# Pinning the neighbour-list work of a sparse attention layer behind the projection's stores and the attention's own products

## The chip, the cores and the metric

The kernel runs on one core of a Trainium2 chip. The metric is the device time of one execution in microseconds. Before the change the median of three runs is 1817.77 us (1814.16 to 1821.57).

## The reference

One layer of a graph network on 4096 nodes with 512 features and 8 heads, followed by a residual layer norm. The adjacency matrix has about 17 neighbours in a row of 4096.

```python
hs = layer_norm(x, ln1_scale, ln1_bias)             # sources
ht = layer_norm(h_target, ln1_scale, ln1_bias)      # targets
q = (ht @ Wq + bq).reshape(T, H, HD) / sqrt(HD)
k = (hs @ Wk + bk).reshape(S, H, HD)
v = (hs @ Wv + bv).reshape(S, H, HD)
logits = where(adj[None] != 0, einsum('thd,shd->hts', q, k), -1e30)
ctx = einsum('hts,shd->thd', softmax(logits), v).reshape(T, D)
ht = layer_norm(ht + ctx @ Wo + bo, ln2_scale, ln2_bias)
y = ht + gelu(ht @ W1) @ W2                         # 512 -> 2048 -> 512
out = layernorm(x + y)
```

All node masks are one. The kernel checks on the chip that its short lists held all neighbours; if not, a dense path follows, which did not run in the executions shown.

## The kernel before, in words

**Lists.** The 4096 targets are 32 tiles of 128 rows. For each tile `edges(i)` (line 717) turns 128 x 4096 adjacency words into lists of neighbours, in four quarters of 1024 columns. A quarter is loaded by SyncE (line 714, 512 KB). ScalarE takes its Sign into bytes and sums the row's degree (line 729). VectorE multiplies pairs of bytes by a row of column numbers (line 734, here "the mask"), and takes the eight largest of five segments (`max`, line 736). After four quarters a decoding follows on VectorE (lines 743 to 760). Quarters are numbered n = 4 i + h here. Quarters of lists 0 to 19 land in the first eight slots of a ring of gathered rows; later ones in two `wide` buffers, so that a load waits for the Sign two quarters before it. Signs go to three `signs` buffers in turn.

**Sorting.** The targets of each half (16 lists) are sorted by degree (`sort`, lines 808 to 858), and their records are scattered to DRAM by 16 indirect transfers of GpSimd (line 854), so that tiles of the sorted order have nearly equal numbers of neighbours, 11 to 39 slots.

**Projection.** `project` normalizes the sources, transposes them on TensorE and multiplies each tile of 128 by Wk and Wv (line 930, 16 matmuls of 512 columns). ScalarE copies both results to a row tile (line 932) and stores it to the DRAM tensor `kvd` (line 936, a transfer issued by ScalarE's queue). `newest` holds that store's instruction, and `latest` a piece of the last row's tile.

**Attention.** For each tile of the sorted order `front` (line 983 on) gathers the targets and makes q. The neighbours' rows k|v are gathered from `kvd` slot by slot by GpSimd (line 967), up to three slots in a step. A step is: q times k on VectorE (line 1220), the sum over each head, the logits (line 1225), exp on ScalarE (1229 or 1238), v times the weights for two slots on VectorE (line 1184) and for the third on ScalarE (eight products, `by_scalar`, line 1204, whose last one becomes `newest`), and the sum over slots by transposing matmuls on TensorE (line 1192). `finish` normalizes and projects by Wo; for a group of two tiles it ends in `h2T` (line 1147). The groups are one tile, then 15 pairs, then one tile.

**Feed-forward.** `feed(g)` multiplies by W1 (line 1325), takes gelu (1328) and multiplies by W2 (1334) once the group's h2T is there, while attention goes on with the next group. `end` does the last layer norm, and GpSimd scatters the rows out (line 1302).

**What sets the order.** The parts are Python generators, woven by `_weave`: each yields a cost, and the one with the least sum goes on. A yield of `None` means that the generator waits. In the first weave there are the projection (7.8 a row), the first half's lists with their sort (2 a quarter, 4 a decoding) and `fill`, which starts once the first half is through and makes five lists of the second half. In the second weave there are attention (60 a pair of tiles in all), feed-forward (60 a pair), and `other_lists`, which begins at 40 and goes on with the remaining 11 lists at 1.5 times those costs, then sorts the second half. This gives the order in which the instructions are written. The framework then puts the instructions of each engine in an order of its own: by when it reckons that their operands are there, and by the written order among those that are ready. An instruction whose operands come early can so be moved far ahead of its place. `tc.issue_after(ins)` forbids that for the instructions written in its block on the engine of `ins`: they are put behind `ins` in that engine's queue. It adds no wait.

Of the kernel before, what the change touches and what calls it, by code (L numbers as in the profile page):

```python
# [1 line left out]

# [441 lines left out]
def adj_resnorm_kernel(  # L444
# [33 lines left out]
    nc = tc.nc  # L478
# [54 lines left out]
    with tc.tile_pool(name="keep", bufs=1) as keep:  # L533
# [17 lines left out]
        with ExitStack() as late:  # L551
# [157 lines left out]
            def quarter(i, h):  # L709
# [4 lines left out]
                nc.sync.dma_start(a, adj[i * P:(i + 1) * P, h * QW:(h + 1) * QW])  # L714
                return a

            def edges(i):

                part = 1 if i >= NA else 0
                rec = Rs[part][:, i - PARTS[part][0], :]  # L720
                cand = lp.tile([P, SEG, 8], U16, name="cand", bufs=2)
                for h in range(NQ):
                    n = i * NQ + h
                    while len(adjs) < min(n + 2, NT * NQ):
                        adjs.append(quarter(*divmod(len(adjs), NQ)))
                    a, adjs[n] = adjs[n], None

                    sg = turn_of("signs", signs)
                    nc.scalar.activation(sg, a, AF.Sign, accum_out=dpart[:, i, h:h + 1])  # L729
                    ahead = min(n + DEEP - 1, n + 3 + n // 2)  # L730
                    while len(adjs) < min(max(n + 3, min(ahead, RINGED * NQ)), NT * NQ):
                        adjs.append(quarter(*divmod(len(adjs), NQ)))
                    wd = sg.bitcast(U16)
                    nc.vector.tensor_tensor(wd, wd, lio, ALU.mult)
                    for s, (w0, w1) in enumerate(SEGS):
                        nc.vector.max(cand[:, h * SQ + s, :], wd[:, w0:w1])  # L736
                    if h == 1:
                        keep_rest()
                    if h % 2 and moms:
                        moments(moms.pop(0))  # L740
                    yield 2.0
                dec = dec_w
                nc.vector.tensor_single_scalar(dec[:, 0], cand, 255, op=ALU.bitwise_and)
                nc.vector.tensor_single_scalar(dec[:, 1], cand, 8, op=ALU.logical_shift_right)
                gid = lp.tile([P, 2 * SEG, 8], F32, name="gid")
                dec = dec.rearrange("p b s e -> p (b s) e")
                off = segoff.rearrange("p b q s -> p (b q s)")
                nc.vector.scalar_tensor_tensor(gid, dec, 0.0,
                                               off.unsqueeze(2).to_broadcast([P, 2 * SEG, 8]),
                                               op0=ALU.is_gt, op1=ALU.mult)  # L750
                nc.vector.tensor_add(gid, gid, dec)
                flat = gid.rearrange("p s e -> p (s e)")
                for r in range(RE // 8):
                    top = rec[:, E0 + r * 8:E0 + (r + 1) * 8]
                    nc.vector.max(top, flat)  # L755
                    if r + 1 < RE // 8:
                        nc.vector.match_replace(flat, top, flat, 0.0)
                held.append((rest_d[i * P:(i + 1) * P, :], flat))
                has = lp.tile([P, MAXE], F32, name="ehas")
                nc.vector.tensor_scalar(has[:, :RE], rec[:, E0:E0 + RE], 0.0, 0.0, op0=ALU.is_gt,  # L760
                                        op1=ALU.add, accum_out=cnt[:, i:i + 1])
                yield 4.0
# [198 lines left out]
                        yield cost  # L961


            recs, tqs, h2Ts, done, ready, latest, newest = {}, {}, {}, set(), [], [], []

            def gather(dst, table, idx):
                nc.gpsimd.indirect_dma_start(  # L967
# [199 lines left out]
            def attention():  # L1167


                tails, pend = [], []  # L1170

                def advance():
                    go_on()
                    for t in list(tails):
                        if next(t, StopIteration) is StopIteration:
                            tails.remove(t)

                def values(i, j0, n, kv, p, cps, after):

                    m = n - 1 if n == S else n
                    v4 = kv[:, :m, D:].rearrange("p j (h d) -> p j h d", h=H)
                    nc.vector.tensor_tensor(v4, v4, p[:, j0:j0 + m, :].unsqueeze(3)  # L1184
                                            .to_broadcast([P, m, H, HD]), ALU.mult)
                    slots = list(range(n))
                    if m > 1 and i >= NA:
                        nc.vector.tensor_add(kv[:, 0, D:], kv[:, 0, D:], kv[:, 1, D:])
                        slots.remove(1)
                    for j in slots:  # L1190
                        for c in range(KC):
                            nc.tensor.matmul(cps[:, c, :], kv[:, j, D + c * P:D + (c + 1) * P], ident,  # L1192
                                             is_transpose=True, start=j0 + j == 0 and c == 0,
                                             stop=j0 + n == TILES[i][1] and j == slots[-1],
                                             skip_group_check=True)
                    if after is not None:
                        tails.append(after)

                def by_scalar(kv, lg):
                    pa = sp.tile([P, H], F32, name="pa")  # L1200
                    nc.scalar.activation(pa, lg[:, S - 1, :], AF.Exp)
                    for hd in range(H):
                        v = kv[:, S - 1, D + hd * HD:D + (hd + 1) * HD]
                        newest[:] = [nc.scalar.mul(v, v, pa[:, hd:hd + 1]).ins]  # L1204

                request(0)
                yield 0.0
                k = 0
                for group in GROUPS:
                    hs = []  # L1210
                    mv = sp.tile([P, 2, 2], F32, name="mv2")
                    cost = 0.5 * UNIT * len(group) / 2 / sum(TILES[i][1] for i in group)
                    for i in group:
                        cps = ps.tile([P, KC, P], F32, name="cps", bufs=2)
                        while k < len(SG) and SG[k][0] == i:
                            _, j0, n = SG[k]
                            while i not in tqs:
                                step(fronts, i)
                            kv, tq = kvs.pop(k), tqs[i]
                            nc.vector.tensor_tensor(kv[:, :n, :D], kv[:, :n, :D],  # L1220
                                                    tq[:, :D].unsqueeze(1).to_broadcast([P, n, D]),
                                                    ALU.mult)
                            lg = sp.tile([P, S, H], F32, name="lg")
                            latest[:] = [lg[:, 0, 0:1]]
                            nc.vector.tensor_reduce(lg[:, :n, :],  # L1225
                                                    kv[:, :n, :D].rearrange("p j (h d) -> p j h d", h=H),
                                                    AX.X, ALU.add)
                            if j0 > 0:
                                nc.scalar.activation(p[:, j0:j0 + n, :], lg[:, :n, :], AF.Exp)  # L1229
                            advance()  # L1230
                            yield cost * n
                            if pend:
                                values(*pend.pop())
                                request(k)
                            advance()
                            if j0 == 0:
                                p = sp.tile([P, MAXE, H], F32, name="p", bufs=1)
                                nc.scalar.activation(p[:, :n, :], lg[:, :n, :], AF.Exp)
                            if n == S:
                                by_scalar(kv, lg)  # L1240
                            last = j0 + n == TILES[i][1]
                            after = finish(i, p, cps, group, hs, mv) if last else None
                            pend.append((i, j0, n, kv, p, cps, after))
                            yield cost * n
                            k += 1
                values(*pend.pop())
                while tails:
                    advance()
                    yield 3.0
                verdict()  # L1250
# [131 lines left out]
            UNIT = 60.0  # L1382

            ed = all_edges()
            steps = NQ + 1
            both = NG
            order = list(range(NG))
            proj = project(order, first_x)
# [31 lines left out]
            def fill():  # L1420
# [1 line left out]
                while not ready:  # L1422
                    yield None
                yield 9.0
                for cost in _take(ed, FILL * steps):
                    yield cost

            att = attention()
            _weave((projections(), 0), (prepare(), 0), (fill(), 0))
# [57 lines left out]
```

## Time and profile before

| | |
|---|---|
| median of three runs | 1817.77 us |
| profiled execution | 1817.49 us |
| its span, first to last instruction | 1815.5 us |
| TensorE matmuls | 1677.8 us busy (92%) |
| VectorE | 1436.5 us busy (79%) |
| ScalarE | 1224.1 us busy (67%) |
| GpSimd | 982.2 us busy (54%) |
| Signs, line 729 | 128 of 1056 ns, 134.9 us busy; 100.0 us idle before them |
| masks, line 734 | 128 of 411 ns, 52.2 us busy; 21.7 us idle before them |
| maxima, line 736 | 640 of 252 ns, 131.8 us busy |
| granted TensorE clock, mean | 0.967 |

In the profile PE is TensorE's matmuls, PEld its weight loads, DVE is VectorE, ACT ScalarE, POOL GpSimd, SP SyncE; a q after the engine marks its sequencer, which issues transfers and waits. L729 is line 729. A row of the timeline is start, length, engine, line, operation, output and inputs, count, and in brackets the engine's idle time before it and what ended it. A row of windows gives, for a stretch of the span, its length, the busy time of each engine with the number of its instructions, the granted clock as a share, the busy share of the 16 DMA engines and what they moved. Most of the ring's views are named kv, so a Sign reads kv<-kv.

### The profile page before, as it was taken

How to read it: one execution, taken by the hardware profiler on the slowest of the kernel's cores; microseconds unless marked ns; L12 is line 12 of the kernel's file. 1: busy time of each engine (PE TensorE's matmuls, PEld its weight loads, DVE VectorE, ACT ScalarE, POOL GpSimd, SP SyncE). 2: the span in 40 equal slices, each digit the busy share in tenths (PEclk: the TensorE clock that was granted, in tenths of full speed). 3: DMA queues.
4: the chain of work that ended last, by engine and by line, in shares of the span. 5: the costliest groups of instructions: out<-in, count | busy, mean ns of one | idle time of the engine just before them, and what ended most of it. 6: DMA issues, size and time to landing. Idle time of an engine off the chain costs nothing. (4 is left out here: it accounts for less than half of the span.)

```text
span 1815.5 us, 22973 instructions
## 1 busy us (share of the span) xinstructions
PE 1677.8 (92%) x7030; PEld 1097.9 (60%) x7030; DVE 1436.5 (79%) x2660; ACT 1224.1 (67%) x3121; POOL 982.2 (54%) x834
## 2 busy tenths in 40 slices
PE   7989984597999979999999989999999999999997
PEld 3434442465766656766776757666666666666664
DVE  6989876899999837777978989978878797988200
ACT  5767654487987736766778868877777676787311
POOL 1000144656566676766678788867575665763101
PEclk9999996698999989999999999999999999999998
DMA  9999968989887557777878878787776776774000
GB/s 344 366 380 372 344 198 319 404 287 332 271 305 256 201 173 243 258 255 267 273 263 302 293 260 295 249 285 250 241 266 222 248 251 238 244 248 153 18 6 26
DMA packets 140269, 463.26 MB, mean 255 GB/s; under 512 B 16500, under 2 KB 21672, under 8 KB 140136
## 3 DMA queue, kind: packets, MB, share of 16 engines
q0 software_dynamic: 96656, 342.64, 55.8%
q1 hardware_dynamic: 35664, 95.98, 15.0%
q10 hardware_dynamic: 7816, 23.08, 3.3%
q8 instruction: 58, 0.95, 0.2%
q14 instruction: 75, 0.61, 0.1%
HBM read 430.75 MB, written 30.89 MB: 254 GB/s over the span
## 5 line engine op out<-in xcount | busy, mean ns | idle before, releaser
L967 POOL DMA_INDIRECT kv<-kvd,rec x603 | 758.1, 1257 | 347.5 <-PE cps L1192 139.7
L1334 PE MATMUL po<-w,gt 128*128 128x512 f32 x1024 | 466.4, 598 | 16.2 <-ACT gt L1328 16.2
L1325 PE MATMUL pf<-h2T,w 128*128 128x256 f32 (+1 forms) x2176 | 465.9, 368 | 0.1
L1325 PEld LDWEIGHTS pf<-h2T,w 128*128 128x128 f32 x2176 | 389.3, 191 | 64.5 <-issue 20.3
L1220 DVE TENSOR_TENSOR kv<-kv,tq 128x1536 f32<-128x1536 f32 (+2 forms) x211 | 351.6, 1675 | 68.3 <-DMA kv<-kvd,rec 56.2
L1204 ACT ACTIVATE kv<-kv,pa 128x64 f32<-128x64 f32 x1520 | 391.0, 336 | 4.3
L1225 DVE TENSOR_REDUCE lg<-kv 128x24 f32<-128x1536 f32 (+2 forms) x211 | 350.1, 1666 | 1.4
L1334 PEld LDWEIGHTS po<-w,gt 128*128 128x128 f32 x1024 | 188.8, 192 | 212.4 <-issue 194.3
L1192 PEld LDWEIGHTS cps<-ident,kv 128*128 128x128 f32 x2008 | 240.2, 145 | 109.4 <-issue 59.2
L1192 PE MATMUL cps<-ident,kv 128*128 128x128 f32 x2008 | 264.5, 280 | 44.1 <-DVE kv L1184 24.5
L1184 DVE TENSOR_TENSOR kv<-kv,p 128x1024 f32<-128x1024 f32 (+1 forms) x211 | 251.0, 1193 | 22.8 <-ACT p L1229 20.3
L687 POOL TENSOR_TENSOR n_rs<-n_ve,mhalf 128x2 f32<-128x2 f32 (+2 forms) x51 | 50.8, 997 | 329.1 <-DVE n_ve L680 165.3
L729 ACT ACTIVATE kv<-kv 128x1024 uint8<-128x1024 int32 x128 | 134.9, 1056 | 100.0 <-DMA kv<-in_adj_dram 51.7
L1328 ACT ACTIVATE gt<-pf 128x512 f32<-128x512 f32 x128 | 76.4, 597 | 93.8 <-PE pf L1325 75.8
L1328 ACT ACT_TABLE_LOAD x104 | 133.4, 1283 | 1.7
L736 DVE MAX8 cand<-kv 128x8 uint16<-128x103 uint16 (+1 forms) x640 | 131.8, 252 | 0.8 <-DVE R L755 0.2
L930 PE MATMUL pq<-wk,h2T 128*128 128x512 f32 x256 | 120.8, 616 | 12.1 <-ACT tq L932 7.2
L1012 PE MATMUL t<-wq,tq 128*128 128x512 f32 x256 | 118.2, 605 | 5.6 <-ACT tq L1006 5.6
L930 PE MATMUL pq<-wv,h2T 128*128 128x512 f32 x256 | 115.5, 594 | 6.4 <-ACT kv L729 3.0
L1229 ACT ACTIVATE p<-lg 128x24 f32<-128x24 f32 (+2 forms) x179 | 39.2, 219 | 113.0 <-DVE lg L1225 88.8
L1116 PE MATMUL t<-wo,rb 128*128 128x512 f32 x256 | 115.2, 592 | 0.0
L930 PEld LDWEIGHTS pq<-wk,h2T 128*128 128x128 f32 x256 | 48.9, 197 | 69.9 <-issue 55.2
(160 smaller groups left out, 1582.2 us busy)
## 6 DMA issues: line engine op xcount, KB each, us to landing
kv<-in_adj_dram SPq DMA_DIRECT2D x128, 512.0 KB
kvd<-tq ACTq DMA_DIRECT2D x24, 512.0 KB
kv<-kvd,rec POOLq DMA_INDIRECT x603
kv<-in_L_gnn_h_target_dram SPq DMA_DIRECT2D x32, 256.0 KB
kv<-in_x_dram SPq DMA_DIRECT2D x15, 512.0 KB
rest_d<-gid SPq DMA_DIRECT2D x32, 160.0 KB
w<-in_L_gnn_W_dram SPq DMA_DIRECT2D x4, 1024.0 KB
kvd<-kv ACTq DMA_DIRECT2D x8, 512.0 KB
```

The source lines that it names most:

```text
L729: nc.scalar.activation(sg, a, AF.Sign, accum_out=dpart[:, i, h:h + 1])
L736: nc.vector.max(cand[:, h * SQ + s, :], wd[:, w0:w1])
L930: nc.tensor.matmul(pkv, hT[:, kc, j * P:(j + 1) * P], w[:, kc, :], start=kc == 0, stop=kc == KC - 1)
L967: nc.gpsimd.indirect_dma_start(out=dst, out_offset=None, in_=table[:, :], in_offset=bass.IndirectOffsetOnAxis(ap=idx, axis=0))
L1184: nc.vector.tensor_tensor(v4, v4, p[:, j0:j0 + m, :].unsqueeze(3) .to_broadcast([P, m, H, HD]), ALU.mult)
L1192: nc.tensor.matmul(cps[:, c, :], kv[:, j, D + c * P:D + (c + 1) * P], ident, is_transpose=True, start=j0 + j == 0 and c == 0, stop=j0 + n ...
L1204: newest[:] = [nc.scalar.mul(v, v, pa[:, hd:hd + 1]).ins]
L1220: nc.vector.tensor_tensor(kv[:, :n, :D], kv[:, :n, :D], tq[:, :D].unsqueeze(1).to_broadcast([P, n, D]), ALU.mult)
L1225: nc.vector.tensor_reduce(lg[:, :n, :], kv[:, :n, :D].rearrange("p j (h d) -> p j h d", h=H), AX.X, ALU.add)
L1325: nc.tensor.matmul(pf[:, k, :], w1[(f0 + k) // KC][:, kc, (f0 + k) % KC * P:((f0 + k) % KC + 1) * P], h2T[:, kc, :w], start=kc == 0, stop= ...
L1328: nc.scalar.activation(gt, pf, AF.Gelu_apprx_tanh)
L1334: nc.tensor.matmul(po[j], gt[:, k, j * P:(j + 1) * P], w2[(f0 + k) // KC][:, (f0 + k) % KC, :], start=False, stop=f0 + k == FC - 1, skip_g ...
```

## The change

Three things are done. The Sign of a quarter of the second half's lists (16 to 31) is put behind `newest`, the newest k|v store or the last of ScalarE's newest eight products at the point where the Sign is written. Each mask is put behind `logits`, the newest logits instruction (empty until attention is written). And `fill` makes three of its five lists as before, and the other two after the last k|v row has been written. A quarter's step is split in two yields, 1 + 1 for the second half's lists and 0 + 2 for the first half's, so that other work can be written between a Sign and its mask; the counts of steps follow (9 a list in place of 5).

```diff
+            def behind(ins):
+                return tc.issue_after(ins[-1]) if ins else nullcontext()
+
             def edges(i):
...
                     sg = turn_of("signs", signs)
-                    nc.scalar.activation(sg, a, AF.Sign, accum_out=dpart[:, i, h:h + 1])
+                    with behind(newest if i >= NA else []):
+                        nc.scalar.activation(sg, a, AF.Sign, accum_out=dpart[:, i, h:h + 1])
                     ahead = min(n + DEEP - 1, n + 3 + n // 2)
                     while len(adjs) < min(max(n + 3, min(ahead, RINGED * NQ)), NT * NQ):
                         adjs.append(quarter(*divmod(len(adjs), NQ)))
+                    yield 0.0 if i < NA else 1.0
                     wd = sg.bitcast(U16)
-                    nc.vector.tensor_tensor(wd, wd, lio, ALU.mult)
+                    with behind(logits):
+                        nc.vector.tensor_tensor(wd, wd, lio, ALU.mult)
...
-                    yield 2.0
+                    yield 2.0 if i < NA else 1.0
...
-            recs, tqs, h2Ts, done, ready, latest, newest = {}, {}, {}, set(), [], [], []
+            recs, tqs, h2Ts, done, ready, latest = {}, {}, {}, set(), [], []
+            newest, logits = [], []
...
-                            nc.vector.tensor_reduce(lg[:, :n, :],
-                                                    kv[:, :n, :D].rearrange("p j (h d) -> p j h d", h=H),
-                                                    AX.X, ALU.add)
+                            logits[:] = [nc.vector.tensor_reduce(
+                                lg[:, :n, :], kv[:, :n, :D].rearrange("p j (h d) -> p j h d", h=H),
+                                AX.X, ALU.add).ins]
...
-            steps = NQ + 1
+            steps = 2 * NQ + 1
...
-                for cost in _take(ed, FILL * steps):
-                    yield cost
+                yield from _take(ed, (FILL - 2) * steps)
+                while not latest:
+                    yield None
+                yield from _take(ed, 2 * steps)
```

More of the change, by code (lines that the diff above doesn't have):

```diff
@@ L1 @@
-from contextlib import ExitStack
+from contextlib import ExitStack, nullcontext
 import concourse.bass as bass
```

## The prediction

> **What bounds the kernel now.** I read the busy shares first, then the 40 slices, then busy time in windows cut at the events of the start-up, then the timeline of ScalarE and GpSimd around the last k|v row.
>
> ```profile
> PE 1677.8 (92%) x7030; PEld 1097.9 (60%) x7030; DVE 1436.5 (79%) x2660; ACT 1224.1 (67%) x3121; POOL 982.2 (54%) x834
> PEclk9999996698999989999999999999999999999998
> ```
>
> TensorE is busy 92% of the span; 138 us of it are idle. Where they lie, by windows:
>
> ```profile
> core 0: us, PE busy (x) PEld busy (x) DVE busy (x) ACT busy (x) POOL busy (x), PEclk, DMA share, GB/s
> 203.00:291.00 88.00, 67.44 (x176) 29.76 (x174) 68.37 (x291) 51.33 (x97) 23.89 (x27) 0.95 0.76 254
> 291.00:373.00 82.00, 44.00 (x182) 31.59 (x182) 65.70 (x105) 40.05 (x132) 56.28 (x46) 0.68 0.96 364
> 373.00:446.00 73.00, 63.16 (x344) 45.80 (x345) 71.38 (x149) 56.66 (x155) 46.23 (x41) 0.91 0.91 320
> 446.00:571.00 125.00, 123.51 (x561) 86.38 (x561) 123.19 (x279) 109.92 (x269) 68.72 (x57) 1.00 0.83 284
> ```
>
> TensorE loses 20.6, 38.0 and 9.8 us in the first three rows, 68 of its 138. From 446 us, where the second group's h2T (line 1147) is ready and its feed-forward starts, TensorE has 98.8% busy in the fourth row and stays near that to the end (1087 of 1126 us after 690). So a gain has to move that point, 446, which I call X; what moves X moves the end one for one. What sets X is VectorE: its gaps are 19.6, 16.3 and 1.6 us in the three rows, 37.5 in all, and from 337 to 446 it has almost none. All of VectorE's work up to X (205.5 us) is done in order, so X is 203 plus that work plus those gaps.
>
> Now the end of the projection, ScalarE's timeline:
>
> ```profile
> 279.25 1.06 ACT L729 ACTIVATE kv<-kv 128x1024 uint8<-128x1024 int32 x1 [2.39 <-DMA kv<-in_adj_dram]
> 280.21 0.19 ACT L729 ACTIVATION_READ_ACCUMULATOR kv<-kv 128x1 f32 x1
> 280.31 0.56 ACT L932 COPY kv<-pq 128x512 f32<-128x512 f32 x1
> ...
> 288.93 1.06 ACT L729 ACTIVATE kv<-kv 128x1024 uint8<-128x1024 int32 x1 [2.57 <-DMA kv<-in_adj_dram]
> 289.89 0.19 ACT L729 ACTIVATION_READ_ACCUMULATOR kv<-kv 128x1 f32 x1
> 289.99 0.57 ACT L932 COPY kv<-pq 128x512 f32<-128x512 f32 x1
> 290.58 0.33 ACTq L936 DMA_DIRECT2D kvd<-kv  x1
> ```
>
> The copies of k and v (line 932) stand behind Sign operations (line 729) that wait for adjacency to land. Over 203 to 300 us Signs waited 23.3 us for that and 10.0 for VectorE's maxima. Numbering Signs in order of time, quarters 84 to 92 (lists 21 to 23) run before the last k|v store at 290.58, although the code writes them inside the attention loop. The gathers wait for that store:
>
> ```profile
> 292.63 0.95 POOL L967 DMA_INDIRECT xt<-in_x_dram,tags  x1 [0.31 <-issue]
> 296.58 0.94 POOL L967 DMA_INDIRECT kv<-kvd,rec  x1 [3.00 <-DMA rest_d<-gid]
> ```
>
> The releaser named there is only the last to land; a gather reads all of kvd, whose last store left 6.0 us earlier.
>
> [...] the copy at 280.31 starts as the Sign in front of it, which had idled ScalarE for 2.39 us, is done. [...] weight loads are only 69% busy from 446 to 571, so VectorE's 98.6% in that row is as likely a limit, and I count losses there too.
>
> **The change part by part.**
>
> *Nothing is added to compute.* The yields split one step in two of the same total cost; for lists 0 to 15 the first half costs 0, so their order stays. The added dependencies are order only. Instructions added: none, 0 us. No table load comes with a Sign in the trace (no line 729 row of that kind).
>
> *Signs of lists 16 to 20 behind k|v stores.* By the costs of the planner, source row k is written at 7.8 k, the filling lists from 207 on, so quarters 64 to 75 are pinned behind the stores of rows 26 to 30, and lists 19 and 20 (quarters 76 to 83) behind the last, row 31. Before, quarter 64 ran at 203 and quarter 83 at 257. This frees ScalarE for the projection. Unblocked rows took about 7.3 us in TensorE (line 930 groups start at 46.7, 54.4, 61.3, 69.0, 75.9). Row 23 starts at 204.8; row 31 would start at 204.8 + 8 x 7.3 = 263.2, end 7.2 later (16 matmuls, two runs of 3.60), and its store leave at about 271 in place of 290.6: 19.6 earlier. The record chain has room: its 16 scatters run 243 to 263, records load at 268 to 271, targets' rows from 272; without list work in front of the sort it should be some us earlier. I take first gather 6.0 after the store, first product 11.5 after that (296.58 to 308.06 now): 288.5 in place of 308.1. Were the record chain not earlier, the first product would come near 295.
>
> *Loads.* Each load of a quarter needs its buffer, so loads slip with the Signs on SP's queue: nothing else waits there but the 160 KB stores of the rest. Quarters 86 to 97, 12 x 0.5 MB = 6 MB, leave the start-up and go behind it. At the 364 GB/s of the second row that is 16 us of transfer, taken from a stretch where gathers waited 11.0 us in four places, and put where the share is 0.91 to 0.96.
>
> *Signs and masks of lists 21 to 31 behind products and logits.* They start where the code writes them, planner time 40, which is the second product row of tile 1. Before, quarters 84 to 98 had run ahead, 258 to 328 us; by 383 us the lead was used up and lists went at the written pace. Up to X (second h2T, planner time 135) the written order masks quarters up to 105; the trace has 107 by 446.8. So the work before X falls by two quarters. A quarter costs 0.41 (line 734) and 5 x 0.206 (line 736), a list's decoding 132.6/32 = 4.1 us (lines 743 to 760), 2.5 a quarter in all; consecutive instructions overlap, and counted without overlap it is 89 us for 43 quarters, 2.1. Gain: 2 x 2.1 = 4.
>
> *VectorE's gaps after.* From 203 to 288.5 there is work for 20 quarters, 42 us, and the sort and small parts, 9: 34.5 us of gap, 15 more than now up to 291. From there the start-up: 16.3 us of gap now, of which 10.1 lie in 291 to 308 and vanish; of the other 6.2 I keep 4. Then 1.6. Sum 40.1 against 37.5: 2.6 lost. The 19.6 us by which attention starts earlier are thus paid back almost whole: list work that had filled VectorE's empty time moves into its full time.
>
> *Coupling.* Now masks follow Signs by 5 to 10 us (462.43 to 471.3 for quarter 111). After it, a Sign stands behind eight products, so it ends 0.2 + 2.0 + 1.25 = 3.5 us after the logits, and a VectorE at 98% may wait for it at the mask. The trace has no such pair to time. Lower bound 0, the other operations in between (1.2 us values, 1.76 products, 1.74 logits) cover 3.5; upper, 0.5 us for each of 44 quarters, 22 us. I take 0.03 to 0.1 each, 1 to 4, as the cover suffices on paper: 3 us. Queued behind such a mask are products and logits of the next slots, and TensorE's transposes wait for those.
>
> Sum: -4 + 2.6 + 3 = +1.6, less about 2 for fewer load waits of ScalarE between 383 and 456 (9 us there, nearly all covered): 0. The profiled execution took 1817.49 us (span 1815.5 and 2.0 around it), the median of the three runs is 1817.77, so the two bases are the same. I predict 1817. Half a per cent, 9 us, is what a measurement of this kernel can tell from no change.
>
> **Rivals.**
>
> *The start-up gain is kept (faster).* If lists after the change run late against the written order, so that before X VectorE does attention only, the 19.6 us stay, less 3: about 1800. For it: 337 to 373 shows VectorE doing attention alone, and no consumer needs the second half's lists before tile 16, near 1015 us. Against: the pinned masks keep their written rank, and the 446 to 571 row has no free VectorE time to take them later (1.8 us).
>
> *Masks stall VectorE (slower).* In 337 to 571 each of the 44 quarters waits for its Sign, 0.5 us each, 22 us, less the 3 counted: about 1836. It decides from 0.27 us each (12 us). For it: ScalarE is 78 to 88% busy there, with 1.28 us table loads and gelus that wait for TensorE in the same queue. Against: the cover above.
>
> *It does not do what it says:* if the stores are not earlier, since something else holds the last rows, lists still lose their early places; about 1822 to 1830, a part of the slower case. And in the 636 to 690 row 10 us of TensorE time are lost behind the second sort's scatters on GpSimd; another order may shift that by 5 either way.
>
> **How the numbers follow.** No change 0.40 (its own range 1807 to 1828: most of it within 9 us, 0.03 below, 0.04 above), kept gain 0.25, slower by stalls or by stores that are not earlier 0.35, of which 0.02 fall within 9 us. So faster 0.28, same 0.35, slower 0.37. For 8 in 10 the range takes in both other cases' centres: 1795 to 1840.
>
> **What would show it.** The last k|v store near 271 and the first product near 288 show the start-up step; Signs of quarters 84 on after 320 show the pins; X between 440 and 452 shows the repayment; VectorE's waits for line 729 at line 734 (18.9 us now) show the coupling. I am wrong if X moves by over 10 us, or if TensorE's idle after X changes by as much.

## The result and the profile after

The changed kernel takes 1834.42 us (1829.49 to 1835.9) beside 1816.01 for the kernel before in the same comparison: a ratio of 1.0097, 95% interval 1.0076 to 1.0117. Repeated later beside the experiments it took 1825.4, ratio 1.0066 (1.0042 to 1.009). It is slower by 0.7 to 1.0%, where no change was forecast. The profiled execution shown here took 1833.78 us, its span is 1832.0.

The busy shares and the granted clock of the kernel after, from its page:

```profile
PE 1687.5 (92%) x7030; PEld 1102.9 (60%) x7030; DVE 1439.8 (79%) x2660; ACT 1223.7 (67%) x3119; POOL 977.9 (53%) x834
PEclk9999996788999999999999999999999999999999
```

Nothing was added: the instruction counts are the same but for two on ScalarE. TensorE is idle 6.8 us longer (144.5 in place of 137.7), and the same 7030 matmuls are recorded as 9.7 us longer, at a mean granted clock of 0.960 in place of 0.967. No run separates the clock from the rest. It does not rank the kernels below: the masks-only kernel, which is faster than the kernel before, has 1689.3 us of matmuls. The experiments are about the idle time. The windows, cut at the same points as before:

```profile
core 0: us, PE busy (x) PEld busy (x) DVE busy (x) ACT busy (x) POOL busy (x), PEclk, DMA share, GB/s
203.00:291.00 88.00, 78.40 (x204) 36.12 (x203) 47.76 (x181) 43.21 (x84) 34.51 (x38) 0.94 0.64 220
291.00:373.00 82.00, 32.66 (x142) 24.36 (x141) 73.25 (x161) 38.89 (x124) 43.08 (x37) 0.65 0.95 362
373.00:446.00 73.00, 61.02 (x331) 43.17 (x329) 71.66 (x162) 52.87 (x139) 41.35 (x34) 0.92 0.84 300
446.00:571.00 125.00, 117.43 (x515) 82.00 (x516) 118.97 (x271) 104.28 (x260) 69.14 (x52) 0.95 0.80 276
```

In the first row TensorE gains 11 us (78.40 in place of 67.44): the projection does end earlier. VectorE loses 20.6 in the same row (47.76 in place of 68.37), gets 7.6 back in the second, and loses 4.2 in the fourth. TensorE gives its gain back in the second row (32.66 in place of 44.00) and loses 6.1 in the fourth. X, the second group's h2T, comes at 453.8 in place of 446.2; the third and fourth come 13.9 and 16.6 later than before, and from there the distance stays at 15 to 17 to the end.

The end of the projection, ScalarE's timeline after:

```profile
274.19 0.59 ACT L938 COPY kv<-pq 128x512 f32<-128x512 f32 x1 [2.26 <-PE pq L936]
274.81 0.33 ACTq L942 DMA_DIRECT2D kvd<-kv  x1
277.13 1.52 ACT L1006 ACTIVATE tq<-tq,rec 128x512 f32<-128x512 f32 x2 [2.35 <-DVE rec L1002]
278.56 1.04 ACT L733 ACTIVATE kv<-kv 128x1024 uint8<-128x1024 int32 x1
```

The last copy now waits for TensorE's product and for no Sign, and the last store leaves at 274.81, 15.8 us earlier. But the Signs of quarters 76 to 83 (lists 19 and 20) all start after it, at 278.56 to 296.51; before, quarter 83's ran at 257. The gathers after:

```profile
277.44 0.98 POOL L974 DMA_INDIRECT xt<-in_x_dram,tags  x1 [13.88 <-DVE tags L1005]
278.73 0.95 POOL L974 DMA_INDIRECT xt<-in_x_dram,tags  x1 [0.30 <-issue]
279.98 0.99 POOL L974 DMA_INDIRECT kv<-kvd,rec  x1 [0.30 <-issue]
```

The first neighbours are gathered at 279.98, 16.6 us earlier than before. The first product on them starts only 1.4 us earlier. VectorE's timeline after shows why:

```profile
288.70 0.69 DVE L1024 SCALAR_TENSOR_TENSOR tq<-t,bqr 128x512 f32<-128x512 f32 x1 [2.41 <-issue]
289.31 0.92 DVE L742 MAX8 cand<-kv 128x8 uint16<-128x103 uint16 x5
...
302.73 0.43 DVE L740 TENSOR_TENSOR kv<-kv,lio 128x512 uint16<-128x512 uint16 x1 [0.35 <-issue]
304.20 1.76 DVE L742 MAX8 cand<-kv 128x8 uint16<-128x103 uint16 x10 [1.05 <-DVE kv L740]
305.88 0.67 DVE L1024 SCALAR_TENSOR_TENSOR tq<-t,bqr 128x512 f32<-128x512 f32 x1
306.47 0.19 DVE L749 TENSOR_SCALAR kv<-cand 128x160 uint16<-128x160 uint16 x1
306.58 0.20 DVE L750 TENSOR_SCALAR kv<-cand 128x160 uint16<-128x160 uint16 x1
306.69 1.75 DVE L1227 TENSOR_TENSOR kv<-kv,tq 128x1536 f32<-128x1536 f32 x1
```

Tile 0's q (line 1024) is there at 289.4. Between it and the first product (line 1227) stand the last maxima and the decoding of list 19, the masks and maxima of list 20 with the start of its decoding, and tile 1's q. The product shows no wait of its own: it stands in line, behind the masks of quarters 82 and 83, which run at 301.97 and 302.73 and whose Signs start only at 294.1 and 296.5. When its gathered slots had landed this trace does not tell; the repeat below bears on that.

Later in the start-up, what VectorE waited for between 306 and 600 us; first before, then after (columns: waiter, releaser, us in total, times, longest):

```profile
DVE kv L1220 <- DMA kv<-kvd,rec: 11.0, 4, 5.2
```

```profile
DVE kv L740 <- ACT kv L733: 5.0, 4, 1.8
```

Before, products (line 1220 then) waited for gathers and no mask waited for a Sign; after, masks wait for Signs and no product for a gather. In sum VectorE does not wait longer in this stretch after the change (8.7 us in place of 18.5 over all releasers), so these lines show the kind of wait and not its price; for that the parts have to be run apart. The median time from a Sign's start to its mask's fell from 6.4 us (quarters 84 to 106) and 11.3 (107 to 127) to 2.5 and 2.8.

### The profile page after: what moved, and what is told of

Same layout as the page of the kernel before. It is cut to its first block, busy times and chain, and to the rows that moved or that the text cites. A ratio compares the mean times of both kernels' runs of the same rounds, so it can differ in the third digit from the quotient of the medians.

```text
span 1832.0 us, 22947 instructions
## 1 busy us (share of the span) xinstructions
PE 1687.5 (92%) x7030; PEld 1102.9 (60%) x7030; DVE 1439.8 (79%) x2660; ACT 1223.7 (67%) x3119; POOL 977.9 (53%) x834
## 5 line engine op out<-in xcount | busy, mean ns | idle before, releaser
L1332 PEld LDWEIGHTS pf<-h2T,w 128*128 128x128 f32 x2176 | 391.6, 192 | 64.1 <-issue 19.6
L1191 DVE TENSOR_TENSOR kv<-kv,p 128x1024 f32<-128x1024 f32 (+1 forms) x211 | 251.3, 1194 | 25.4 <-ACT p L1236 21.3
L742 DVE MAX8 cand<-kv 128x8 uint16<-128x103 uint16 (+1 forms) x640 | 128.1, 251 | 4.0 <-DVE kv L740 2.5
```

Source lines behind the costliest of these rows:

```text
L1332: nc.tensor.matmul(pf[:, k, :], w1[(f0 + k) // KC][:, kc, (f0 + k) % KC * P:((f0 + k) % KC + 1) * P], h2T[:, kc, :w], start=kc == 0, stop= ...
```

## The experiments

"Filling lists" are 16 to 20, "later lists" 21 to 31. The experiments ran in four batches, each with the kernel before beside it (1813.87, 1814.7, 1817.26 and 1818.33 us), and the ratios are to that (to 1816.01 for the kernel after); times of steps come from one profiled execution each. Kernels are named by what is pinned, and the diffs are against the kernel after. "Product" is the first product's start, X the second group's h2T, and idle is VectorE's from 203 to 690 us (487 less its busy time in that window).

| kernel | ratio (95%) | last store | product | X | idle | span |
|---|---|---|---|---|---|---|
| before | 1 | 290.6 | 308.1 | 446.2 | 77.4 | 1815.5 |
| after | 1.0097 (1.0076 to 1.0117) | 274.8 | 306.7 | 453.8 | 85.9 | 1832.0 |
| after, repeated | 1.0066 (1.0042 to 1.009) | 273.7 | 298.1 | 447.4 | 82.5 | 1819.7 |
| filling Signs | 1.0013 (1.0001 to 1.0026) | 271.1 | 295.2 | 441.8 | 75.4 | 1811.8 |
| later Signs, masks | 1.0025 (1.0014 to 1.0035) | 272.8 | 285.0 | 440.9 | 79.2 | 1816.0 |
| all Signs | 1.0071 (1.0048 to 1.0095) | 272.9 | 297.1 | 447.1 | 86.4 | 1825.8 |
| masks | 0.997 (0.9958 to 0.9982) | 275.4 | 289.7 | 435.6 | 72.9 | 1808.9 |
| masks, again | 0.9966 (0.9946 to 0.9985) | 275.0 | 288.3 | 433.1 | 74.0 | 1812.2 |
| after, 19 and 20 free | 1.0033 (1.0022 to 1.0044) | 274.8 | 289.2 | 442.5 | 79.8 | 1818.6 |
| after, 16 to 18 free | 1.0048 (1.0031 to 1.0065) | 271.3 | 296.1 | 446.1 | 87.3 | 1823.4 |
| masks, later Signs a step older | 0.9971 (0.9961 to 0.9982) | 272.9 | 286.1 | 433.3 | 73.0 | 1815.0 |
| nothing pinned | 1.0006 (0.9993 to 1.0019) | 289.6 | 307.2 | 446.4 | 78.3 | 1816.2 |
| masks, old filling order | 0.9946 (0.9931 to 0.9961) | 275.1 | 286.5 | 434.4 | 73.8 | 1805.3 |
| filling Signs, masks | 1.0041 (1.0029 to 1.0052) | 274.7 | 306.9 | 452.0 | 84.8 | 1827.5 |

In most rows the span is 1736 to 1739 plus the idle time of VectorE; the exceptions are the kernel after (1746), the one with filling Signs and masks (1743), the one a step older (1742, in a profiled execution at the upper end of its times) and the old filling order (1732). So the gaps of VectorE in the start-up account for most of the differences over the fourteen, not all; between the two kernels shown they grow by 8.5 us and the span by 16.5.

**The parts of the change one by one.** The Signs of the filling lists alone:

```diff
-                    with behind(newest if i >= NA else []):
+                    with behind(newest if NA <= i < NA + FILL else []):
...
-                    with behind(logits):
+                    with behind([]):
```

> Only the Signs of the five filling lists (16 to 20) are pinned; later Signs and all masks are free. Theory A (list work is moved out of VectorE's empty time; VectorE's gaps up to the second h2T set the end): the last store leaves near 275 as after the change, VectorE still stands empty before it, but lists 21 on fill the start-up, so 1816 to 1822. Theory B (masks that wait for Signs in the attention stage make the loss, the fill pins are a gain): the coupling is gone and the earlier store is kept, 1803 to 1810.

The Signs of the later lists, with the masks:

```diff
-                    with behind(newest if i >= NA else []):
+                    with behind(newest if i >= NA + FILL else []):
```

> Only lists 21 to 31 are pinned, Signs and masks; the filling lists are free. Theory A: lists 21 to 24 move into the attention stage (about 11 us), the stores come earlier since no late Sign stands before them, so half of the loss or less, 1818 to 1826. Theory B: all of the loss, 1830 to 1836.

All Signs and no masks:

```diff
-                    with behind(logits):
+                    with behind([]):
```

> All Signs pinned as in the change, masks free. Theory A: the masks follow their Signs anyway, so the same as the change, 1830 to 1837. Theory B: with masks free VectorE need not stand before one whose Sign is late, so at least half of the loss is gone, 1816 to 1826.

The masks and no Signs:

```diff
-                    with behind(newest if i >= NA else []):
+                    with behind([]):
```

> Masks of lists 21 on pinned behind the logits, all Signs free. Theory A: the three sign buffers fill and the lists then keep the written pace, so the work of lists 21 to 24 moves all the same: 1820 to 1830. Theory B: Signs lie ahead of their masks again, no coupling: 1814 to 1820.

They took 1815.87, 1817.4, 1827.75 and 1809.12 us. Neither theory came through whole: the first two lie just under A's ranges, the third between both, the fourth under both. Each of the four has the early store, 271 to 276, so the filling Signs' pins and the masks' pins each bring it without the other. The masks alone made a gain that neither theory had: 1809.12 us beside 1813.87. With the later Signs pinned as well it is 8.3 us more. So I formed a third theory, C: filling pins put the list work of lists 19 and 20 in front of the first product; later pins put each Sign so near to its mask that the mask waits; mask pins by themselves are a gain.

VectorE's waits from 285 to 571 us in the kernel with later Signs and masks, and then in the one with masks alone:

```profile
DVE kv L740 <- ACT kv L733: 11.0, 6, 2.3
DVE kv L1227 <- DMA kv<-kvd,rec: 8.8, 5, 2.4
```

```profile
DVE tq L1024 <- PE t L1019: 13.4, 2, 12.8
DVE kv L1227 <- DMA kv<-kvd,rec: 2.3, 3, 1.1
```

Masks waited 11.0 us for Signs in the first and not at all in the second (its 12.8 lies ahead of the first product, with no list work to do). One such wait followed back, in the kernel with later Signs and masks: SyncE's, ScalarE's and VectorE's timelines.

```profile
365.49 1.37 SPq L714 DMA_DIRECT2D kv<-in_adj_dram  x2
```

```profile
365.37 1.04 ACT L733 ACTIVATE kv<-kv 128x1024 uint8<-128x1024 int32 x1
...
372.35 1.06 ACT L733 ACTIVATE kv<-kv 128x1024 uint8<-128x1024 int32 x1 [3.94 <-DMA kv<-in_adj_dram]
```

```profile
373.53 0.43 DVE L740 TENSOR_TENSOR kv<-kv,lio 128x512 uint16<-128x512 uint16 x1 [1.84 <-ACT kv L733]
```

A load into a wide buffer can go only when the Sign that reads that buffer is done. The Sign of quarter 92 was done at 365.37, and the load of quarter 94 was issued at 365.49; the Sign of 94 idled ScalarE for 3.94 us until the data had landed, started at 372.35, and the mask waited for that. Of the six waits four are of this kind; in the other two the Sign had not waited for a load. Loads between 355 and 400 us took 4.9 to 8.2 us to land, where the trace tells it. That the load is the larger part is argued from these rows and not shown: a third wide buffer would test it, and no run here has one.

**Which of the filling lists.** The change with lists 19 and 20 free, and with 16 to 18 free:

```diff
-                    with behind(newest if i >= NA else []):
+                    with behind(newest if i >= NA and i - NA not in (FILL - 2, FILL - 1) else []):
```

> The change, but the Signs of lists 19 and 20 (quarters 76 to 83) are not pinned. Theory C (behind the last store these eight quarters stand in VectorE's queue before the first product, and the loads of the last two wait for their buffers): first product 288 to 294 in place of 306.7, 1818 to 1824. Theory D (it is the emptiness left by lists 16 to 18 that costs): first product after 300, 1827 to 1834.

```diff
-                    with behind(newest if i >= NA else []):
+                    with behind(newest if i >= NA + FILL - 2 else []):
```

> The change, but the Signs of lists 16 to 18 (quarters 64 to 75) are not pinned, those of 19 and 20 are. Theory C: first product 296 to 306, 1826 to 1834. Theory D: first product before 292, 1816 to 1821.

With lists 19 and 20 free the first product comes at 289.2, 10.8 after the first gather, and the ratio falls to 1.0033. With them alone pinned it comes at 296.1, 21.3 after. Both products are where C put them; the second kernel's time, 1823.46, is a little under C's 1826, and the rival put beside C is not met. So the two lists behind the last row make the late product, and the three before them hardly matter for it.

**Room between Sign and mask.** The filling lists free, and each later Sign behind the products of the step before the newest:

```diff
-                    with behind(newest if i >= NA else []):
+                    with behind(older if i >= NA + FILL else []):
...
+                    older[:] = newest
```

> Filling lists free, masks pinned as in the change, and each later Sign is pinned behind the products of the step before the newest one, so that it can run one step (about 6 us) ahead of its mask. Theory C (a Sign right behind the newest products makes its mask wait, 8 us over the lists): VectorE's waits for Signs go from 11.0 us to under 2, 1808 to 1812. Rival (the loss of the Sign pins is list work that comes later, not waiting): 1815 to 1819, as with the pin behind the newest.

1809.86 us: C's time. Compared with the same pins one step later (1817.4, in another batch) it wins back 8 to 10 us, by the times and by the ratios (0.9971 beside 1.0025); no mask waits for a Sign after 285 us, and the median from Sign to mask is 9.1 us. Keeping Signs near their written place costs nothing, keeping them next to their masks does.

**The change again.**

> The changed kernel once more, beside the others on their chip: 1830 to 1836, first product 304 to 309 if the 9 us by which VectorE's list work there runs slower than with free masks belongs to the program, 296 to 299 if it was that one execution.

1825.4 us, under the 1830 to 1836 expected; the ratio is 1.0066, and its interval overlaps that of the first comparison. VectorE's timeline of the repeat:

```profile
295.31 0.43 DVE L740 TENSOR_TENSOR kv<-kv,lio 128x512 uint16<-128x512 uint16 x1 [1.83 <-ACT kv L733]
295.65 1.76 DVE L742 MAX8 cand<-kv 128x8 uint16<-128x103 uint16 x10
297.32 0.67 DVE L1024 SCALAR_TENSOR_TENSOR tq<-t,bqr 128x512 f32<-128x512 f32 x1
...
298.13 1.75 DVE L1227 TENSOR_TENSOR kv<-kv,tq 128x1536 f32<-128x1536 f32 x1
```

The order is the same, ten maxima and tile 1's q and then the product, 20.9 us after the first gather in place of 26.7. Tile 0's q is finished at 286.7 in the repeat and at 289.4 in the first profile; from there to the product it is 11.4 and 17.3 us. The three gathered slots of the step had landed at 285.6 in the repeat, as far as the trace tells, so that nothing but the queue was left to wait for. With lists 19 and 20 free VectorE idled 1.38 us for a gather before the first product, 10.8 us after the first gather; in the repeat it is not idle before it, at 20.9. So the queue makes 11.4, and the other 5.9 of the first profile are a slow stretch that not every execution has (see the end).

**What makes the gain of the masks.** Nothing pinned, so that only the writing order of lists 19 and 20 and the split yields stay; and the masks pinned with the old writing order:

```diff
-                    with behind(newest if i >= NA else []):
+                    with behind([]):
...
-                    with behind(logits):
+                    with behind([]):
```

> Neither Signs nor masks are pinned; what stays of the change is that lists 19 and 20 are written after the last k|v row, and the split yields. If the mask pins make the gain that the masks-only kernel showed (they keep lists 21 on from running ahead), this kernel behaves like the kernel before: last k|v store 286 to 293, first product 303 to 310, ratio 0.999 to 1.002. Rival: the gain came from the later writing of lists 19 and 20; then the last store leaves at 270 to 278, the first product comes by 291, and the ratio is 0.996 to 0.998.

```diff
-                    with behind(newest if i >= NA else []):
+                    with behind([]):
...
-                yield from _take(ed, (FILL - 2) * steps)
-                while not latest:
-                    yield None
-                yield from _take(ed, 2 * steps)
+                yield from _take(ed, FILL * steps)
```

> Only the masks are pinned, and all five filling lists are written in one go as before the change. If the mask pins make the gain alone, last k|v store 271 to 278, first product by 291, ratio 0.996 to 0.998, as with the later writing. Rival: without the later writing lists 19 and 20 keep standing before the last rows, the store leaves after 283, and the ratio is 0.999 or more.

The writing order alone does nothing that shows (store 289.6, ratio 1.0006); the mask pins alone do it all, and somewhat more than expected (0.9946). ScalarE's Signs and the last store in the kernel with masks and the old order:

```profile
256.33 1.06 ACT L733 ACTIVATE kv<-kv 128x1024 uint8<-128x1024 int32 x1 [3.98 <-DMA kv<-in_adj_dram]
...
263.68 1.06 ACT L733 ACTIVATE kv<-kv 128x1024 uint8<-128x1024 int32 x1
264.73 1.04 ACT L733 ACTIVATE kv<-kv 128x1024 uint8<-128x1024 int32 x1
...
275.05 0.33 ACTq L942 DMA_DIRECT2D kvd<-kv  x1
...
321.86 1.04 ACT L733 ACTIVATE kv<-kv 128x1024 uint8<-128x1024 int32 x1
```

These are quarters 84, 85, 86, and 87 after the store. Three Signs fill the three sign buffers; their masks stand behind the first logits, so the fourth has no buffer until the first of those masks (318.6) is done. In the kernel before, nine went ahead of the last store. A mask's pin thus keeps the Signs out of the projection's way and leaves them their lead: from Sign to mask it is 13.8 us in the median (quarters 84 to 106).

**Do the parts add up?** The filling Signs and the masks, and the masks alone once more beside them:

```diff
-                    with behind(newest if i >= NA else []):
+                    with behind(newest if NA <= i < NA + FILL else []):
```

> The change without the pins on the Signs of the later lists (21 to 31); the Signs of the filling lists (16 to 20) and all masks stay pinned. If the parts add up, the filling pins cost what they cost beside the other pins (0.4 to 0.7% on the masks alone): first product 294 to 300 in place of some 288, no mask waits for its Sign after 310, ratio 1.001 to 1.004. Rival: the later product of the start-up is made good where the later Signs are free, as it seemed in the kernel with the filling pins alone; then the ratio is within 0.1% of the masks-only kernel run beside it.

> The kernel with the masks pinned and all Signs free, a second time: ratio 0.995 to 0.998. It also tells whether writing lists 19 and 20 later costs anything: if the difference to the kernel with the masks pinned and the old writing (0.9946) is real, this one stays at 0.9965 or above.

1825.71 and 1812.31 us: on top of the masks the filling pins cost 0.74%, a little over what was expected. The rival falls. The product came at 306.9, later than expected, with the same slow stretch as in the first profile of the change. The masks' gain came again (0.9966, just over the 0.9965 set as the mark); its interval overlaps that of the old writing order, so whether the later writing of two lists costs 0.2% stays open. No mask waited for a Sign after 306 us, and VectorE had no idle time from X to 571.

So the change is the sum of a gain of 0.3 to 0.5% (masks), a loss of 0.4 to 0.7% (filling Signs) and one of 0.3 to 0.6% (later Signs), counted in this order. The parts overlap: without the masks' pins the filling pins cost next to nothing (1.0013 beside 1.0006 with nothing pinned), as they bring the early store themselves; and with all Signs pinned the masks' pins change nothing that shows (1.0071 without them, 1.0066 and 1.0097 with them). Three kernels beat both kernels shown: the masks pinned alone with the new or the old writing order, and the masks with the later Signs one step older. The best, with the old order, takes 1808.47 us beside 1817.26.

## Why the prediction was wrong

*Last store near 271, first gather 6.0 after it.* Right in the main: 274.8 and 273.7, 15.8 and 16.9 us earlier of the 19.6 forecast, and the gather 5.2 and 3.5 after. The rival that the stores would not be earlier falls.

*"First product 11.5 after that", 288.5.* Wrong, and this is the step that failed: 26.7 and 20.9 after, at 306.7 and 298.1. I took the distance over from the profile of before, where the product waited 5.2 us for the gather and lists 19 and 20 were done. I had myself put quarters 76 to 83 behind the last row, and booked their 17 us or so of VectorE work as filling the gap up to 288.5. But nothing in the pin lets it be done there: the Signs can start only at 278.6, the last two loads only as Signs 80 and 81 free their buffers (286.6 on), and what is then late is queued ahead of the product. With those lists free the distance is 10.8, in the kernels with the early store and no filling pins 8 to 9.

*VectorE's gaps, 40.1 up to X.* 50.3 in the first profile (47.5 before the first product, 2.8 after it), 44.9 in the repeat (39.9 and 5.0). X = 203 + work + gaps is an identity, since a gap is time without work, and could not fail; the gaps were mis-sized by the step above: I had 34.5 before the product and 5.6 after it.

*Two fewer quarters before X, -4.* The size was right, 105 masks and 5.0 us less work, but it is no gain for the end. VectorE had 1.8 us idle from X to 571 before; list work that is put off past X comes due there (the last mask is at 595.8 in place of 570.7). "What moves X moves the end one for one" does not hold where X moves by putting work off: in the two profiles of the masks-only kernel X is 10.6 and 13.1 us earlier than before, and the span 6.6 and 3.3 shorter. Gaps tell more: 39.4 us from 203 to 571 before, 56.4 after, 17.0 more, and the span grew by 16.5. That this comes out so close is luck; in the repeat it is 8.8 more and the span 4.2, and over the fourteen profiles the span less these gaps lies between 1768 and 1777.

*Coupling, +3.* Under-sized: the later pins cost 8.3 us beside the masks, about 0.19 for each of 44 quarters, within the bounds (0 to 22) and under the 0.27 from which I let the rival decide alone. The cover I had worked out, 3.5 us from logits to the end of a Sign, left out the load: I counted the bytes of slipped loads, and not that a load starts when a Sign frees its buffer (365.49 after 365.37 in the rows above) and lands 4.9 to 8.2 us later. That this is what the cover lacked is argued, as said above; that the nearness of Sign and mask costs the time is shown by the kernel one step older.

*Loads.* The slipped loads do not show as more traffic: 0.95 and 362 GB/s in the second row, 0.96 and 364 before. The 11.0 us that I booked as waits of gathers are waits of products for gathers.

*The rivals.* The stalled masks had the right sign for the change, 1836, with 8 us by their mechanism and not 22; the rest came from the queue before the first product, which no rival named. The kept gain does exist, at 0.3 to 0.5%, where only the masks are pinned: 4.8 to 8.8 us of the 15 by which the store is earlier.

*TensorE's idle after X* grew by 4.5 us up to 690 (12.7 to 17.2) and not after it (38.2 to 36.0). So neither of the two signs of being wrong that I had named came: X moved by 7.6 us and this idle time by 2.3. The other 6.7 of the 16.5 us are matmul time after X: 11 more matmuls are left there, and the granted clock is 0.95 in place of 1.00 in the fourth row. What share the clock has stays open.

## What to carry to other kernels

An order-only pin added no instruction here (7030 matmuls and 2660 instructions of VectorE before and after) and no wait that it names, but it moved what depended on the pinned instruction: its result's consumers in another engine's queue (list work stood between the first product and its q, 17.3 and 11.4 us earlier), and the transfer that its buffer releases (issued at 365.49, with the Sign done at 365.37). When a distance is taken over from the profile of before ("11.5 us after the gather"), list what will now stand between the two ends in the consumer's queue. To keep a producer from running ahead, it was better in this kernel to pin the consumer and let the few buffers between them limit the lead (0.9946 to 0.997 of the time before) than to pin the producer next to its consumer (1.0025 with the later Signs pinned too).

## What was not expected of the hardware

In the first profile of the change, and in that of the filling Signs with the masks, VectorE idled between list instructions that follow one another on the same engine, with no other engine named as the releaser ("remote" is a wait whose end the trace puts down to no instruction). VectorE's timeline of the kernel with filling Signs and masks:

```profile
296.59 0.09 DVE L763 MATCH_VALUE_LOAD gid<-R,gid 128x8 int32 x1 [2.69 <-remote]
...
298.01 0.27 DVE L742 MAX8 cand<-kv 128x8 uint16<-128x103 uint16 x1 [0.87 <-issue]
300.11 0.49 DVE L761 MAX8 R<-gid 128x8 int32<-128x320 f32 x1 [1.83 <-remote]
...
302.90 0.18 DVE L766 TENSOR_SCALAR_CACHE_REDUCE ehas<-R 128x24 f32<-128x24 int32 x1 [2.13 <-remote]
```

These four gaps are 7.5 us; in the first profile of the change they are 5.9 at the same four lines. The repeat has none there. In all three the DMA engines were busy over 90% of the time from 287 to 305 us, and GpSimd's gathers take the same time (10.7 and 10.6 us in these 18, 10.6 in the repeat from 284 to 298), so that neither load alone brings it about. The cause stays open. It fell between the first gather and the first product both times. With three profiles it is not known how often it comes, nor how much of the spread between executions is due to it.
